# Moving block 0's products with W1 from the preparation into the keys' stage of a graph-attention kernel

## The chip, the cores and the metric

The kernel runs on one core of a Trainium2 chip. The metric is the time of one execution on the device in microseconds (us), the median of three runs. A profiled execution gives the times of single instructions. The engines are named as in the profile: PE (TensorE, matrix products and transposes; PEld is its weight load), DVE (VectorE), ACT (ScalarE), POOL (GpSimd, which issues the gathers) and SP (SyncE, which issues most other transfers). Each engine works through its own list of instructions in order and waits where a semaphore tells it to.

## The reference

Two layers of relational graph attention over a graph of 3125 nodes with 768 features and 53125 edges of three types, then a residual sum and a layer norm. One layer, cut to what matters:

```python
xr = jnp.einsum('nd,rdf->rnf', x, W)          # W: three relations, 768 x 768
oi, oj = xr[etype, dst], xr[etype, src]
alpha = jax.nn.leaky_relu(oi @ q + oj @ k, 0.2)
m = jax.ops.segment_max(alpha, dst, num_segments=n_nodes)
e = jnp.exp(alpha - m[dst])
z = jax.ops.segment_sum(e, dst, num_segments=n_nodes)
a = e / (z[dst] + 1e-16)
msg = (a[:, :, None] * oj.reshape(-1, heads, out_ch)).reshape(-1, heads * out_ch)
out = jax.ops.segment_sum(msg, dst, num_segments=n_nodes) + b
```

Layer 1 has four heads and the weights W1, q1, k1; an ELU follows it. Layer 2 has one head. At the end: `_layernorm(x + out)`. The edges come sorted by their target node.

## The kernel before, in words

The nodes are cut into 25 blocks of 128 (`NB`); the last holds 53 nodes. The edges are cut into slots of 128, at most 14 for block 0 and 17 for every other block, 422 in all (`NK`). A product with float32 accuracy is made of three products of split numbers, so that one "group" (128 nodes by half of one relation's 768 columns) takes 6 x 3 = 18 matmuls. Everything is written under a manual schedule: the order of the program is the order of each engine's list.

The stages:

1. **Preparation** (`prepare`, `weights_kq`, `nodes_kq`). W1 is loaded in 18 pieces of 384 KB, each split into a high and a low part (`wH`, `wL`) and turned on PE (L260) for the product of W1 with q1 and k1, which gives the small matrix `wk` (product L282, placing L320). Then the 25 blocks of x are loaded, turned and multiplied with `wk`, which gives every node's key and query numbers (product L282, placing L372); the keys go to a table in DRAM, `kt1` (L379). Two blocks make one chunk. In before, chunk 0 is block 0 alone, and its turned parts are kept (`t0H`, `t0L`), so that `first` (L396) can make block 0's products with W1 in 18 parts of six matmuls each. `early` and `fills` say how many parts are made at which step. The rows that come of it go from three buffers ("row") to the table `tab1`, by ACT's copies (L403) and ACT's queue (L406). `Buffers` deals six buffers of `share` out to the pieces of W1, the blocks of x and these rows in the order of `waiting`; a load is issued on SP (L173, L178) when a buffer comes free. `prepare` writes the edges' tables in small steps that `more` puts between these.

2. **The keys' stage** (`phase1`). POOL gathers the keys of every slot from `kt1` (L461, 422 gathers of 128 rows). The gathers of one block need its index: a transpose on PE (L540), then DVE (L545 to L570). PE adds the scores' helpers per block (L613, L642, L659), and beside that makes the products of x with W1, group by group (`d_group`, L698), after turning the block (`d_turn`, L675). ACT copies a group's result to a row buffer (L713) and SP stores it to `tab1` (L715). Six groups make one block; the last four blocks go together, relation by relation (the tail), since their turned parts are kept in other buffers. `ev` says at which group number each helper step is done: six groups to a block, with a fixed distance for each step. Every sixth matmul of a group also waits for a certain gather ("an even load"), so that the groups are spread over the gathers. The node blocks come again from DRAM for this, one at a time (`x_load`, one buffer `xr`).

3. **Layer 1's sums** (`phase2`) gather rows from `tab1` and need the whole table. **Layer 2** (`phase3`) follows.

A fallback kernel for other edge lists is in the file, and is not run for these inputs.

Of the kernel before, what the change touches and what calls it, by code (L numbers as in the profile page):

```python
# [8 lines left out]
F32 = mybir.dt.float32  # L9
# [40 lines left out]
def kernel(  # L50
# [95 lines left out]
    class Buffers:  # L146


        def __init__(self):
            w = [("W", i) for i in range(R * DT)]  # L150
            self.waiting = w[:10] + [("x", 0)] + w[10:] + [("x", b) for b in range(1, NB)]
            self.spare = list(range(6))
            self.at = {}

        def __getitem__(self, key):
            t = share[self.at[key]]
            return t if key[0] == "row" else t[:, :D]

        def want(self, *key):
            self.waiting.insert(0, key)  # L160
            self.go()

        def free(self, *key):
            self.spare.append(self.at.pop(key))
            self.go()

        def go(self):
            while self.waiting and self.spare:
                key = self.waiting.pop(0)
                self.at[key] = self.spare.pop(0)  # L170
                kind, i = key
                if kind == "W":
                    nc.sync.dma_start(self[key], l1["W"].rearrange("r (t p) f -> (r t) p f", p=P)[i])  # L173
                elif kind == "x":
                    n = min(P, N - i * P)
                    if n < P:
                        V.memset(self[key], 0.0)
                    nc.sync.dma_start(self[key][:n], x[i * P:i * P + n, :])  # L178
# [162 lines left out]
    def nodes_kq(buf, pre, work, psum, bank, wk, kqs, wH, wL, qq, more, edges_ready):  # L341

        NCH = NB // 2 + 1

        def chunk(m):

            return (2 * m - 1, min(2, NB + 1 - 2 * m)) if m else (0, 1)

        def turn(m):
            b, nb = chunk(m)  # L350
            pts = transposes(psum, [buf["x", b + c] for c in range(nb)])
            for c in range(nb):
                buf.free("x", b + c)
            if m > 1:
                place(m - 2, prod.pop(m - 2))
            return split_parts(work, pts, nb * P, "t" if m else "t0")

# [26 lines left out]

        def first(i):

            g, i = divmod(i, 3)
            r, c = divmod(g, 2)
            if i == 0 and c == 0:
                buf.want("row", r)  # L390
            if i == 0:
                po[g] = psum.tile([P, 512], F32, name="po", bufs=1)
            tH, tL = got[0][i]
            for t in (2 * i, 2 * i + 1):
                for n, (a, w) in enumerate(((tH, wH), (tH, wL), (tL, wH))):
                    T.matmul(po[g][:, :HALF], a[:, t % 2, :], w[:, r * DT + t, c * HALF:(c + 1) * HALF],  # L396
                             start=(t == 0 and n == 0), stop=(t == DT - 1 and n == 2))
            if i < 2:
                return
            o = buf["row", r]  # L400
            if c == 0:
                G.memset(o.rearrange("p (h f) -> p h f", h=H1)[:, :, F1:CW], 1.0)
            S.copy(o.rearrange("p (h f) -> p h f", h=H1)[:, 2 * c:2 * c + 2, :F1],  # L403
                   po.pop(g)[:, :HALF].rearrange("p (h f) -> p h f", h=2))
            if c == 1:
                nc.scalar.dma_start(tab1[:P * R, :].rearrange("(p r) f -> p r f", r=R)[:, r, :], o)  # L406
                buf.free("row", r)

        got = {}
        prod = {}  # L410
        po = {}
        left = iter(range(6 * R))

        def fill(n):
            for _, i in zip(range(n), left):
                first(i)

        def begin(m):

            if m in (-5, 0):  # L420
                got[len(got)] = turn(len(got))
            fill(early.get(m, 0))


        early = {-4: 1, -3: 1, -2: 1, -1: 1, 0: 2, 1: 1}
        yield begin
        fills = [0] + [1] * 12 + [2, 0]
        for m in range(1, NCH + 2):
            if m >= NCH:
                place(m - 2, prod.pop(m - 2))  # L430
            elif m > 1:
                got[m] = turn(m)
            fill(fills[m])
            if 0 <= m - 1 < NCH:
                prod[m - 1] = product(m - 1, got[m - 1])
            more(1)
            if m == NCH - 3:
                edges_ready()
                x_load(pre, 1)
        yield  # L440
# [78 lines left out]
    def phase1(pre, work, psum, wH, wL, qq):  # L519
# [167 lines left out]

        def d_group(n, b, r, c):

            g, k = divmod(n, 6)  # L690
# [1139 lines left out]
```

## Time and profile before

| | us |
|---|---|
| three timed runs | 2191.54, 2200.53, 2206.43 (median 2200.53) |
| the profiled execution: time, span | 2187.15, 2185.4 |
| busy: PE, DVE, ACT, POOL | 1994.7 (91%), 1528.2 (70%), 1358.0 (62%), 1669.4 (76%) |
| preparation, to the first gather of keys | 0 to 126.18 |
| keys' stage, to the first gather of rows | 126.18 to 702.13 |
| layer 1's sums, to the last store to layer 2's table | 702.13 to 1538 |
| layer 2 | 1538 to 2185.4 |

All numbers of stages are from the profiled execution, counted from the start of its span. A line of the order of time gives the start, the duration, the engine, the line of the program, the operation, output<-inputs, the shapes, the count and, in brackets, how long the engine was idle before and what it waited for. A table of windows gives, for each stretch of time, the busy time of each engine with its number of instructions, the clock granted to PE as a share of its full clock, the share of time in which the 16 DMA engines were busy, and what they moved.

### The profile page before, as it was taken

What the parts mean: (1) busy time and instruction counts of PE and PEld (TensorE: products, weight loads), DVE (VectorE), ACT (ScalarE), POOL (GpSimd) and SP (SyncE); (2) the same over time, 40 slices, a digit from 0 to 9 for tenths busy, and PEclk for the clock granted to TensorE, in tenths of its full rate; (3) what the DMA queues carried; (4) which work ended last, traced back from release to release, by engine and by line L of the source; (5) the groups of instructions that cost most, each with busy time, mean ns of one, the idle gap of its engine ahead of it and who ended that gap; (6) DMA issues with size and microseconds to landing.
All of it is one profiled execution on the core that took longest, in us unless ns stands there. A gap on an engine that the chain in (4) does not pass through costs nothing.

```text
span 2185.4 us, 37792 instructions
## 1 busy us (share of the span) xinstructions
PE 1994.7 (91%) x10953; PEld 1736.7 (79%) x10953; DVE 1528.2 (70%) x4159; ACT 1358.0 (62%) x3095; POOL 1669.4 (76%) x1615
## 2 busy tenths in 40 slices
PE   6979999999987799999999999999488989999887
PEld 5979988898887799999999999999255555555555
DVE  6545445455434999999999999996166666766666
ACT  5412112222111788888888888885378879788886
POOL 4257777777777888888888888884677777777774
PEclk8989999999999899999999999999699999999999
DMA  6555545555547987888788888886789899988882
GB/s 176 185 141 173 192 144 156 179 167 167 176 155 223 315 243 239 245 245 248 234 251 247 244 242 244 240 253 201 253 290 303 302 311 308 310 288 297 288 297 91
DMA packets 156844, 506.06 MB, mean 232 GB/s; under 512 B 43875, under 2 KB 57069, under 8 KB 156628
## 3 DMA queue, kind: packets, MB, share of 16 engines
q0 software_dynamic: 81904, 331.52, 50.2%
q1 hardware_dynamic: 64494, 156.04, 20.7%
q10 hardware_dynamic: 10230, 15.98, 2.2%
q8 instruction: 91, 1.49, 0.3%
q14 instruction: 125, 1.02, 0.1%
HBM read 412.55 MB, written 95.69 MB: 233 GB/s over the span
## 4 chain that ended last, share of the span: by engine, by line
PE 52%; DMA 14%; issue 14%; POOL 13%; DVE 4%; ACT 2%; POOLq 0%; DVEq 0%; SPq 0%; ACTq 0%
PE po L949 21%; PE acc L894 13%; POOL kt L461 9%; DMA G<-ftab,ridx 9%; PE acc L1168 8%; PE po L698 4%; DMA kt<-kt,ridx 2%; POOL G L461 2%; PE bank L282 1%; PE pt L260 1%; DVE L L1157 1%; PE po L396 1%; PE pt L924 1%; POOL share L461 1%; ACT H L1146 1%
## 5 line engine op out<-in xcount | busy, mean ns | idle before, releaser
L861 ACT ACTIVATE H<-share,pall 128x193 fp32r<-128x193 f32 x1672 | 616.9, 447 | 91.2 <-PE acc L894 29.6
L875 DVE SCALAR_TENSOR_TENSOR L<-share,pall,H 128x193 fp32r<-128x193 f32 x1672 | 621.0, 437 | 16.5 <-issue 6.6
L949 PE MATMUL po<-wH,hT 128*128 128x386 f32 (+1 forms) x1800 | 529.6, 339 | 0.0
L461 POOL DMA_INDIRECT G<-ftab,ridx x374 | 424.0, 1134 | 114.0 <-issue 57.9
L461 POOL DMA_INDIRECT share<-ftab,ridx x374 | 428.3, 1145 | 80.5 <-DVE L L875 30.9
L461 POOL DMA_INDIRECT kt<-kt,ridx x374 | 396.8, 1061 | 114.2 <-issue 110.1
L698 PE MATMUL po<-wH,xT 128*128 128x384 f32 x1584 | 439.7, 347 | 12.7 <-ACT share L713 4.8
L1168 PE MATMUL acc<-G,selp 128*128 128x386 f32 x868 | 341.5, 519 | 0.0
L949 PEld LDWEIGHTS po<-wH,hT 128*128 128x128 f32 x1800 | 334.4, 189 | 0.6 <-DVE hT L937 0.5
L698 PEld LDWEIGHTS po<-wH,xT 128*128 128x128 f32 x1584 | 292.8, 190 | 19.8 <-ACT share L713 7.0
L949 PE MATMUL po<-wL,hT 128*128 128x386 f32 (+1 forms) x900 | 304.8, 339 | 0.0
L698 PE MATMUL po<-wL,xT 128*128 128x384 f32 x792 | 269.2, 340 | 0.0
L1157 DVE SCALAR_TENSOR_TENSOR L<-G,p,H 128x772 fp32r<-128x772 f32 x205 | 208.2, 1017 | 57.3 <-ACT H L1146 56.9
L713 ACT COPY share<-po 128x384 f32<-128x384 f32 x144 | 67.9, 478 | 278.7 <-PE po L698 275.2
L894 PE MATMUL acc<-H,sel 128*128 128x386 f32 x836 | 224.9, 350 | 12.1 <-POOL sel L863 10.9
L1168 PEld LDWEIGHTS acc<-G,selp 128*128 128x128 f32 x868 | 163.8, 199 | 81.3 <-issue 17.3
L863 POOL TENSOR_SCALAR sel<-frow,fdl 128x128 fp32r<-128x128 f32 x278 | 216.0, 777 | 12.6 <-PE acc L894 1.8
L894 PE MATMUL acc<-L,sel 128*128 128x386 f32 x836 | 217.3, 341 | 0.0
L1146 ACT ACTIVATE H<-G,p 128x772 fp32r<-128x772 f32 x205 | 189.9, 928 | 0.9 <-DVE p L1122 0.8
L949 PEld LDWEIGHTS po<-wL,hT 128*128 128x128 f32 x900 | 169.8, 189 | 0.0
L894 PEld LDWEIGHTS acc<-H,sel 128*128 128x128 f32 x836 | 148.8, 190 | 23.2 <-POOL sel L863 21.1
L894 PEld LDWEIGHTS acc<-L,sel 128*128 128x128 f32 x836 | 154.8, 191 | 0.2 <-DVE L L875 0.2
(246 smaller groups left out, 2810.1 us busy)
## 6 DMA issues: line engine op xcount, KB each, us to landing
ftab<-share SPq DMA_DIRECT2D x75, 386.0 KB
ftab<-r SPq DMA_DIRECT2D x75, 386.0 KB
share<-in_L_gnn_W_dram SPq DMA_DIRECT2D x36, 384.0 KB
w_d<-w2hl SPq DMA_DIRECT2D x18, 768.0 KB
sT<-dr_d SPq DMA_DIRECT2D x25, 544.0 KB
share<-in_x_dram SPq DMA_DIRECT2D x25, 384.0 KB
xb_d<-share SPq DMA_DIRECT2D x25, 384.0 KB
xr<-in_x_dram SPq DMA_DIRECT2D x23, 384.0 KB
```

What stands on the lines that cost most here:

```text
L260: T.transpose(pt[:, f, c * P:(c + 1) * P], a[:, (2 * i + f) * P:(2 * i + f + 1) * P], ident)
L461: return G.indirect_dma_start(out=to, out_offset=None, in_=tab, in_offset=_index(i[:, j:j + 1]), bounds_check=NP * R - 1, oob_is_err=False)
L698: m = T.matmul(po[:, :HALF], xT[:, s, t, :], w[:, i, sl], start=(n == 0), stop=(n == 3 * DT - 1))
L713: S.copy(to, po[:, :HALF].rearrange("p (h f) -> p h f", h=2))
L861: S.activation(H[:, c], g[:, c], AF.Copy, scale=pall[:, b, j, h:h + 1])
L863: (V if k % 3 == 0 else G).tensor_scalar(sel, row, dl[:, b, j:j + 1], None, op0=ALU.is_equal)
L875: V.scalar_tensor_tensor(L[:, c], g[:, c], pall[:, b, j, h:h + 1], H[:, c].bitcast(F32), op0=ALU.mult, op1=ALU.subtract)
L894: T.matmul(acc[:, c, :HW], sel, a[:, c * HW:(c + 1) * HW], start=(j == 0 and i == 0), stop=(k in ends2 and i == 1), skip_group_check=True)
L949: T.matmul(po[:, :wd], hT[:, k, t, :], w[:, r * DT + t, sl], start=(t == 0 and n == 0), stop=(t == DT - 1 and n == 2))
L1146: S.activation(H, g, AF.Copy, scale=p)
L1157: V.scalar_tensor_tensor(L, g, blk[b]["p"][:, j:j + 1], st[k][1].bitcast(F32), op0=ALU.mult, op1=ALU.subtract)
L1168: T.matmul(acc[:, c, :HW], sel, a[:, c * HW:(c + 1) * HW], start=(j == 0 and i == 0), stop=(k in ends and i == len(parts) - 1))
```

## The change

Block 0 is treated like all other blocks. In the preparation `first`, its parts, its kept tiles and its row buffers are gone, the 18 pieces of W1 are loaded first and then the blocks of x, and the chunks are (0, 1), (2, 3), ..., (22, 23), (24), 13 as before. The last node block has a place of its own, `share[7]`, which is cleared at the start; the loads keep their order, so its load is issued after that of block 23, without a buffer to wait for. In the keys' stage there are 150 groups for 144. The helper steps of a block are placed at 37/6 groups per block (`when`) for 6, and the groups are spread over the gathers by one formula, 23/25 of the matmuls' sixths, for a rule by blocks. The special load and sum that made block 0's residual row are gone, since `d_split` now makes it.

```diff
         def __init__(self):
             w = [("W", i) for i in range(R * DT)]
-            self.waiting = w[:10] + [("x", 0)] + w[10:] + [("x", b) for b in range(1, NB)]
+            self.waiting = w + [("x", b) for b in range(NB)]
             self.spare = list(range(6))
-            self.at = {}
+
+            self.at = {("x", NB - 1): 7}
+            V.memset(share[7], 0.0)
...
         def free(self, *key):
-            self.spare.append(self.at.pop(key))
-            self.go()
+            i = self.at.pop(key)
+            if i < 7:
+                self.spare.append(i)
+                self.go()
 
         def go(self):
             while self.waiting and self.spare:
                 key = self.waiting.pop(0)
-                self.at[key] = self.spare.pop(0)
+                if key not in self.at:
+                    self.at[key] = self.spare.pop(0)
...
-        NCH = NB // 2 + 1
+        NCH = (NB + 1) // 2
 
         def chunk(m):
 
-            return (2 * m - 1, min(2, NB + 1 - 2 * m)) if m else (0, 1)
+            return 2 * m, min(2, NB - 2 * m)
...
-        def first(i):
...
         def begin(m):
 
-            if m in (-5, 0):
-                got[len(got)] = turn(len(got))
-            fill(early.get(m, 0))
-
-
-        early = {-4: 1, -3: 1, -2: 1, -1: 1, 0: 2, 1: 1}
+            if m in (0, 1):
+                got[m] = turn(m)
+
         yield begin
-        fills = [0] + [1] * 12 + [2, 0]
         for m in range(1, NCH + 2):
             if m >= NCH:
                 place(m - 2, prod.pop(m - 2))
             elif m > 1:
                 got[m] = turn(m)
-            fill(fills[m])
-            if 0 <= m - 1 < NCH:
-                prod[m - 1] = product(m - 1, got[m - 1])
+            if m - 1 < NCH:
+                prod[m - 1] = product(m - 1, got.pop(m - 1))
             more(1)
             if m == NCH - 3:
                 edges_ready()
-                x_load(pre, 1)
+                x_load(pre, 0)
...
-                        tc.add_manual_dep(m.ins, gathered[g, (3 * k + n // 6) * slots(g) // 18].name, behind,
+                        tc.add_manual_dep(m.ins, gathered[slot((3 * k + n // 6) * 23 // 25)].name, behind,
                                           reason="an even load")
...
-        d_turn(1)
-        d_split(1)
-        x_load(pre, 2)
+        d_turn(0)
+        d_split(0)
+        x_load(pre, 1)
...
-        groups = [(b, r, c) for b in range(1, GB) for r in range(R) for c in range(2)]
+        groups = [(b, r, c) for b in range(GB) for r in range(R) for c in range(2)]
         groups += [(b, r, c) for r in range(R) for b in range(GB, NB) for c in range(2)]
         ev = {}
+
+        def when(b, d):
+
+            return b * 37 // 6 + d
...
-                ev.setdefault(6 * b + d + (b == 1), []).append((f, b))
+                ev.setdefault(when(b, d) + (b == 1), []).append((f, b))
...
-                if 6 * b + d >= 0:
-                    ev.setdefault(6 * b + d, []).append((f, b))
-        ev[6 * NB - 10].append((lambda b: a_last(), 0))
-        for b in range(2, GB + 1):
-            for d, f, o in ((-8, d_turn, 0), (-7, d_split, 0), (-7, x_next, 1)):
+                if when(b, d) >= 0:
+                    ev.setdefault(when(b, d), []).append((f, b))
+        ev[when(NB - 1, -4)].append((lambda b: a_last(), 0))
+        for b in range(1, GB + 1):
+            for d, f, o in ((-2, d_turn, 0), (-1, d_split, 0), (-1, x_next, 1)):
                 ev.setdefault(6 * b + d, []).append((f, b + o))
...
-            if n == 2:
-                nc.sync.dma_start(share[3][:, :D], x[:P, :])
-            if n == 8:
-                V.tensor_add(share[4][:, :D], share[3][:, :D], b2r)
-                nc.sync.dma_start(xb_d[:P, :], share[4][:, :D])
-            m = n - 6 * (GB - 1)
+            m = n - 6 * GB
```

More of the change, by code (lines that the diff above doesn't have):

```diff
@@ L150, in __init__ @@
             w = [("W", i) for i in range(R * DT)]
-            self.waiting = w[:10] + [("x", 0)] + w[10:] + [("x", b) for b in range(1, NB)]
+            self.waiting = w + [("x", b) for b in range(NB)]
             self.spare = list(range(6))
-            self.at = {}
+            self.at = {("x", NB - 1): 7}
+            V.memset(share[7], 0.0)
         def __getitem__(self, key):
[L156 to L160, printed above, removed]
-            self.go()
+            return share[self.at[key]][:, :D]
         def free(self, *key):
-            self.spare.append(self.at.pop(key))
-            self.go()
+            i = self.at.pop(key)
+            if i < 7:
+                self.spare.append(i)
+                self.go()
         def go(self):
@@ L173, in go @@
                     nc.sync.dma_start(self[key], l1["W"].rearrange("r (t p) f -> (r t) p f", p=P)[i])
-                elif kind == "x":
+                else:
                     n = min(P, N - i * P)
-                    if n < P:
-                        V.memset(self[key], 0.0)
                     nc.sync.dma_start(self[key][:n], x[i * P:i * P + n, :])
@@ L355, in turn @@
                 place(m - 2, prod.pop(m - 2))
-            return split_parts(work, pts, nb * P, "t" if m else "t0")
+            return split_parts(work, pts, nb * P)
         def product(m, parts):
@@ L383, in place @@
                                                      g4[:, c, 1, :, 1, :])
-        def first(i):
[L387 to L407, printed above, removed]
         got = {}
         prod = {}
[L411 to L416, printed above, removed]
         def begin(m):
-            if m in (-5, 0):
-                got[len(got)] = turn(len(got))
-            fill(early.get(m, 0))
-        early = {-4: 1, -3: 1, -2: 1, -1: 1, 0: 2, 1: 1}
+            if m in (0, 1):
+                got[m] = turn(m)
         yield begin
-        fills = [0] + [1] * 12 + [2, 0]
         for m in range(1, NCH + 2):
@@ L686, in d_split, with d_group @@
             nc.sync.dma_start(xb_d[b * P:(b + 1) * P, :], xb)
-        def d_group(n, b, r, c):
-            g, k = divmod(n, 6)
+        def d_group(k, b, r, c):
             po = psum.tile([P, 512], F32, name="po", bufs=2)
```

## The prediction

> **What bounds the kernel now.** I read the page first (PE 91% of the span, POOL 76%, the chain half on PE), then the table of engine times by stage, then the order of time of PE and POOL around the two places that the change touches.
>
> The preparation, from PE's order of time (start, duration, engine, line, output<-inputs, count, idle before):
>
> ```profile
> 72.85 1.47 PE L260 MATMUL pt<-fident,share 128*128 128x128 f32 x12
> 74.25 0.32 PE L372 MATMUL bank<-fident,sm 48*128 48x48 f32 x2
> 74.50 0.44 PE L396 MATMUL po<-wH,t0H 128*128 128x384 f32 x1
> ...
> 75.49 0.34 PE L396 MATMUL po<-wH,t0L 128*128 128x384 f32 x1
> 75.66 0.40 PE L282 MATMUL bank<-tH,wk 128*128 128x256 f32 x2
> ...
> 77.05 1.47 PE L260 MATMUL pt<-fident,share 128*128 128x128 f32 x12
> ...
> 114.50 1.42 PE L260 MATMUL pt<-fident,share 128*128 128x128 f32 x11 [2.68 <-DMA share<-in_x_dram]
> 116.54 0.80 PE L282 MATMUL bank<-tH,wk 128*128 128x256 f32 x2 [0.37 <-ACT g L374]
> 117.14 0.63 PE L282 MATMUL bank<-tL,wk 128*128 128x256 f32 x2
> ```
>
> One pair of node blocks takes 4.20 us (72.85 to 77.05) without a gap: turning, placing, one sixth-part of block 0's products (L396, 74.50 to 75.66, 1.16 us), key product. PE is the bound there. At the end PE waits 2.68 us for the last node block's load.
>
> The same stage by windows (us from the start; busy us of PE, PEld, DVE, ACT, POOL; granted clock; DMA share; GB/s):
>
> ```profile
> 40.00:50.00 10.00, 8.84 (x68) 8.37 (x69) 8.23 (x18) 7.24 (x14) 3.92 (x3) 1.00 0.55 169
> 50.00:60.00 10.00, 9.10 (x73) 8.65 (x72) 9.79 (x17) 6.71 (x14) 5.16 (x5) 1.00 0.54 165
> 70.00:80.00 10.00, 10.00 (x75) 9.38 (x74) 5.34 (x13) 5.64 (x15) 2.82 (x8) 1.00 0.48 148
> 90.00:100.00 10.00, 10.00 (x81) 9.56 (x80) 5.07 (x12) 4.90 (x12) 2.32 (x8) 1.00 0.77 235
> 110.00:120.00 10.00, 6.49 (x41) 5.68 (x40) 4.19 (x10) 3.77 (x9) 0.00 (x0) 0.83 0.17 56
> ```
>
> While W1 is split (40 to 60) DVE is 90% busy too; with the node blocks (70 to 110) only PE is full.
>
> The keys' stage, from POOL's order of time, then PE's:
>
> ```profile
> 126.18 1.11 POOL L461 DMA_INDIRECT kt<-kt,rfirst  x1 [19.20 <-DVE own L567]
> ...
> 634.60 1.00 POOL L461 DMA_INDIRECT kt<-kt,ridx  x1 [0.48 <-DVE lim L556]
> ...
> 700.83 1.00 POOL L461 DMA_INDIRECT kt<-kt,ridx  x1 [0.30 <-DMA ftab<-share]
> 702.13 0.99 POOL L461 DMA_INDIRECT share<-ftab,rfirst  x1 [0.30 <-issue]
> ```
>
> ```profile
> 571.62 0.52 PE L642 MATMUL pa<-fident,al 128*68 128x128 f32 x3 [1.07 <-DVE al L636]
> ...
> 627.25 1.51 PE L675 MATMUL px<-fident,xr 128*128 128x128 f32 x6 [8.24 <-DMA xr<-in_x_dram]
> ...
> 706.46 0.83 PE L642 MATMUL pa<-fident,al 128*68 128x128 f32 x3 [7.69 <-DVE al L636]
> ```
>
> POOL issues 422 gathers of keys without a rest, 1.00 us each and 0.30 between, a few longer: 126.18 to 701.83, 1.364 us apiece. That chain is the stage's length; the next stage's first gather follows at once. PE, paced to it, waits now and then for the gathered keys (571.62) and once for a load. So I count in time after the first gather (t0 = 126.18).
>
> **The preparation.** 18 parts leave, 1.16 us each: 20.9 us of PE at most. Term by term:
> - Ten pair periods, turns 2 to 11. Without its part PE needs 3.04 us; DVE 2.14 (0.25 + 1.89), ACT 2.18 (0.24 + 1.57 + 0.37). DMA: shares of 0.57, 0.48, 0.54, 0.77 and 0.49 in the five windows from 60 to 110 make 28.5 us over 12 pairs, 2.4 each. All below PE. But two loads (786 KB) at 235 GB/s, the best of the windows shown, would take 3.35. I take 1.0 us saved per period: **10.0** (0.85 to 1.16: 8.5 to 11.6).
> - Four W1 periods, 4.64 us (45.13 to 49.77). PE would do with 3.48, DVE's 90% are 4.2. Saved 0.45 to 1.16 each; I take 0.6, as DVE is nearer: **2.5** (1.8 to 4.6).
> - From turn 1 to turn 2 (59.05 to 68.69, 9.64 us, four parts). Then this stretch holds the turn of the first pair too (+1.4), and the waits that the parts covered are bare: sums' copies (0.45 each) and wk's four DVE steps (0.8 at 66.34). Say 7.6: **2.0** (1.0 to 2.7).
> - Block 0's six transposes leave the slow spot at 34.48 (18 in 3.90 us there, 12 in 2.6 by 28.54's rate): **1.2**.
> - The end. The last chunk holds one block (0.75 us for 1.47) and its load no longer waits for a buffer: it follows block 23's load instead of the turn of blocks 19 and 20. 111.55 to 115.84 becomes 0.8 to 1.0: **3.3** (0.7 to 3.6). Without the pause the product after it keeps its clock (2.95 us now, 1.40 elsewhere): **1.0** (0 to 1.5).
>
> Sum 20.0 us, t0 at 106; ends 13 and 25. ACT's six copies (0.52 each), three store issues on ACT's queue, POOL's three memsets (0.1) go as well, all beside PE; so do SP's waits for those stores (9.5 us in the queue's waits). New is a 0.70 us memset on DVE, idle until 11 us: nothing.
>
> A rule to weigh: after the pause of 2.68 us a pair of 256-column matmuls took 0.63 us for 0.40, at a granted clock of 0.83 in that window. [...] Were the clock to fall in five W1 chunks (transposes 2.6 for 1.46, product 2.58 for 1.39), the 20.0 would be 8.
>
> **The keys' stage.** PE gets six groups of 18 matmuls, 3.17 us each (668.51 to 671.68), and one turn (0.82): +19.8. ACT gets six copies (0.48) and a cast (0.80), DVE a subtraction (0.94); its addition for xb replaces L802. SP gets three row stores for two transfers of block 0, in a stage where DMA is half idle. On POOL nothing changes: I cost it 0 (-2 to +3 for longer gathers).
>
> Is there room on PE? From 128.75 to 599.02 it did 120 groups, aux work included, in 22.4 us per six without waits (201.70 to 224.09): 448 us, plus 1.5 at a low clock; some 20 us were waits. With 37/6 groups per block a block costs 22.4 + 3.17/6 = 22.9 us against POOL's 17 x 1.364 = 23.2. It fits, barely: PE stays paced. Block 19's last key is gathered at slot 337, t0 + 463, its scores pass PE at group 122; four groups on, the tail (last four blocks) starts at about t0 + 482, where it was t0 + 472.8.
> The tail itself is the same 24 groups with the same 8.24 us stall: its load is issued when block 23's rows are free, in both. It takes 97.6 us (599.02 to 696.6), so PE ends at t0 + 579.5 for t0 + 570.4. Then a copy (0.7), a store's issue (0.35) and its landing (under 3.6 today, as 702.13 didn't wait): the next stage's first gather at t0 + 583.5 for 575.95, 7.5 late. The scores of block 24 hold ACT until 709.73 anyway (first scaling at 710.20, t0 + 584.0), so less of it counts: I take **+6** (0 if the tail's stall shrinks; 18 if the waits stay and all 19.8 come on top).
>
> [...]
>
> **Sum.** -20.0 + 6 = -14 us; the later stages move along. On the profiled execution: 2187.15 - 14 = 2173. That execution lies under all three timed runs (2191.54 to 2206.43); from their median 2200.53 it is **2186.5**.
>
> **Rivals.**
> 1. Forecast, PE freed in front and nearly full behind: -14, 2186.5. Chance 0.50.
> 2. Another engine takes over in front (DVE in the W1 chunks, loads at 3.35 us): -13 + 6 = -7, 2193.5. For it DVE's 9.79 of 10; against it the 5.07 with node blocks. 0.20.
> 3. The tail gives nothing back: PE's waits swallow all: -20 + 0, 2180.5. For it the 20 us of waits; against it that they lie before the tail. 0.13.
> 4. Slower: PE becomes the bound of the keys' stage. Its place is the index transpose (L540) that frees POOL for the next block: it queues behind more groups. It decides once PE's lag exceeds POOL's lead; at 634.60 the lead is used up already (0.48 for 0.30). Then all 19.8 and the store's tail come through POOL, +20 for -13: +7, 2207.5. Against it: block 22's index is now issued ahead of the stalled turn, and 22.9 is under 23.2. 0.11.
> 5. The change doesn't shorten the preparation, because the loads pace it: only the end's 4 us come, +6: +2, 2202.5. Against it: no PE wait for a load from 29 to 111. 0.06.
>
> The bounds run from -25 to +7, with a few us for the runs' own spread: 2172 to 2207. One per cent (22 us) is about what a measurement of this kernel can tell. Faster by more: the low half of case 3 and the edge of 1: 0.15. Slower by more: the far edge of 4: 0.03. Within: 0.82.
>
> **What would show it.** Right: first gather of keys near 106; pair periods near 3.2 us; no wait before the last turn; 422 gathers again in 576 us; an idle stretch of some 6 us on POOL between the last gather of keys and the first of rows. Wrong: pair periods still near 4 with waits for loads; POOL gaps over 0.3 us before a block's first gather, laid to DVE L556; PE waits for keys gone before the tail.

## The result

The changed kernel takes 2203.86 us (median of 20 runs; 2189.62 to 2218.64 but for one slow run of 2770.47, at a granted clock of 0.65), the kernel before 2195.91 us beside it (20 runs, 2184.96 to 2206.43). The ratio is 1.0043, with a 95% interval from 1.0025 to 1.006: **slower by 9 us** (by the ratio; the medians lie 8.0 us apart), where 14 us of gain were forecast. That is under the one per cent that the forecast's chances called no change, but the sign is wrong and the cause can be found. The profiled execution of the changed kernel took 2206.68 us, its span is 2204.9 us, its mean granted clock 0.958 (0.961 before). Before's profiled execution (2187.15 us) lies 8.8 us under its median, so the two profiles lie 19.5 us apart; about 10 us of that are not in the medians, and I compare stages, not whole spans.

POOL's order of time for the changed kernel (start, duration, engine, line, operation, output<-inputs, count, idle before and releaser):

```profile
117.37 1.11 POOL L424 DMA_INDIRECT kt<-kt,rfirst  x1 [13.01 <-DVE own L530]
...
654.01 0.99 POOL L424 DMA_INDIRECT kt<-kt,ridx  x1 [4.57 <-DVE lim L519]
...
678.21 1.44 POOL L424 DMA_INDIRECT kt<-kt,ridx  x1 [2.25 <-DVE lim L519]
...
699.62 0.99 POOL L424 DMA_INDIRECT kt<-kt,ridx  x1 [0.30 <-issue]
...
709.01 1.00 POOL L424 DMA_INDIRECT share<-ftab,rfirst  x1 [8.40 <-DMA ftab<-share]
```

The preparation got shorter by 8.8 us (126.18 to 117.37), not by 20. From the first gather of keys to the first gather of rows it takes 591.6 us, not 575.95: 15.7 us more, where about 7 were forecast. Together the sums of layer 1 start 6.9 us later (702.13 to 709.01). The gathers of keys now wait twice for an index (4.57 and 2.25 us, "DVE lim"), and the first gather of rows waits 8.40 us for the last store of rows, so PE's last group sets the end of the stage.

**The preparation.** PE's order of time, changed kernel:

```profile
55.91 0.80 PE L280 MATMUL bank<-tH,kqs 128*128 128x256 f32 x2 [4.55 <-DVE g L320]
...
99.05 0.50 PE L280 MATMUL bank<-tH,wk 128*128 128x256 f32 x2 [0.46 <-ACT g L372]
...
100.54 1.47 PE L258 MATMUL pt<-fident,share 128*128 128x128 f32 x12
101.94 0.32 PE L370 MATMUL bank<-fident,sm 48*128 48x48 f32 x2
102.72 0.50 PE L280 MATMUL bank<-tH,wk 128*128 128x256 f32 x2 [0.46 <-ACT g L372]
```

A pair of blocks now takes 3.54 to 3.71 us (once 4.45, with a step of the edges' tables in it), not 3.2. After the placing (L370, 101.94) PE has to wait 0.46 us until ACT has copied its result out of the PSUM tile `bank` (L372), since the next product writes other columns of the same tile. In before the part of block 0 stood in just this place (74.50 to 75.66) and covered the copy. The wait at 55.91 is a new one. What DVE and POOL did just before it:

```profile
46.89 0.18 DVE L320 COPY g<-bank 128x32 f32<-128x32 f32 x1
47.10 5.57 DVE L322 TENSOR_TENSOR w<-g 128x16 f32<-128x16 f32 x1
52.71 0.17 DVE L323 CAST wk<-w 128x16 fp32r<-128x16 f32 x1
```

```profile
45.48 0.53 POOL L200 DMA_DIRECT2D dr_d<-share  x1 [4.64 <-DVE share L225]
46.02 6.62 POOL L303 TENSOR_TENSOR wL<-share,wH 128x768 fp32r<-128x768 f32 x4
```

DVE's addition of 128 x 16 numbers lasts 0.18 us elsewhere and 5.57 us here. It ends (52.67) where POOL's run of four subtractions ends (52.64). The copy that PE waited for (L320, at 55.67) stands behind this addition in DVE's list. The run is that long because POOL stood behind a store for 4.64 us and the pieces had piled up. After PE's pause of 4.55 us its granted clock is 0.74 and 0.75 in two windows, and 1.00 in the ones before and after (us from the start; busy us of PE, PEld, DVE, ACT, POOL; granted clock; DMA share; GB/s):

```profile
40.00:50.00 10.00, 8.34 (x68) 7.43 (x68) 9.79 (x17) 8.43 (x17) 5.35 (x5) 1.00 0.52 151
50.00:60.00 10.00, 5.00 (x28) 4.43 (x28) 9.16 (x16) 2.81 (x6) 2.64 (x2) 0.74 0.64 204
60.00:70.00 10.00, 7.90 (x47) 7.31 (x46) 7.13 (x20) 3.68 (x7) 0.00 (x0) 0.75 0.41 141
```

The transposes of one chunk took 2.82 us in that stretch, 1.53 before it.

**The keys' stage.** The longest waits of PE from the first gather of keys to its last group (us in total, times, longest), before:

```profile
PE pa L642 <- DVE al L636: 14.0, 11, 2.1
PE px L675 <- DMA xr<-in_x_dram: 8.9, 2, 8.2
```

and in the changed kernel:

```profile
PE px L638 <- DMA xr<-in_x_dram: 13.0, 2, 7.6
PE po L660 <- ACT share L675: 4.4, 9, 0.8
PE pa L605 <- DVE al L599: 3.9, 5, 1.6
```

The waits for scores ("al") fell from 14.0 to 3.9 us; those for a node block's load rose from 8.9 to 13.0. The turns of the last blocks in PE's order, and the loads on SP's queue, changed kernel:

```profile
595.01 0.82 PE L638 MATMUL px<-fident,xr 128*128 128x128 f32 x6
...
611.36 1.54 PE L638 MATMUL px<-fident,xr 128*128 128x128 f32 x6 [5.42 <-DMA xr<-in_x_dram]
...
620.46 0.87 PE L638 MATMUL px<-fident,xr 128*128 128x128 f32 x6
...
636.56 1.51 PE L638 MATMUL px<-fident,xr 128*128 128x128 f32 x6 [7.59 <-DMA xr<-in_x_dram]
```

```profile
600.30 0.82 SPq L453 DMA_DIRECT2D T<-ed_d  x1
601.33 0.71 SPq L497 DMA_DIRECT2D w<-ed_d  x1
...
602.65 0.37 SPq L468 DMA_DIRECT2D xr<-in_x_dram  x1
...
627.14 0.30 SPq L468 DMA_DIRECT2D xr<-in_x_dram  x1
```

The load for the turn at 611.36 is issued 7.6 us after the turn before it (595.01), the last one 6.7 us after (620.46); before, the last one took 4.5 us (611.49 to 616.03). In the order of the program, index and scan steps stand ahead of that block's split (L646), and only the split frees the buffer. On DVE, where the first of these steps waits for PE:

```profile
599.13 0.22 DVE L541 TENSOR_SCALAR s_all<-pT,s_all 128x1 f32<-128x1 f32 x1 [2.45 <-PE pT L539]
...
600.14 0.94 DVE L646 TENSOR_TENSOR xT<-px,xT 128x768 fp32r<-128x768 f32 x1
```

The late issue is not the whole of the first wait. In before the load for the turn at 603.00 is issued just as late (589.38 to 597.56, 8.2 us), and PE does not wait for it: 13.6 us lie between the two turns there, 2.07 of them a wait for scores, and 10.9 here, without the wait. And here the load itself takes 8.66 us to land, against 4.37 for the next one in before (issued at 606.99). On SP's list it stands right behind two loads of the edges' tables (L453, L497). That these made it slow is not shown.

### The profile page after: what moved, and what is told of

It reads as the page before. It is cut to its first block, busy times and chain, and to the rows that moved or that the text cites. A ratio compares the mean times of both kernels' runs of the same rounds, so it can differ in the third digit from the quotient of the medians.

```text
span 2204.9 us, 37814 instructions
## 1 busy us (share of the span) xinstructions
PE 2003.9 (91%) x10959; PEld 1741.7 (79%) x10959; DVE 1529.6 (69%) x4159; ACT 1358.5 (62%) x3096; POOL 1685.5 (76%) x1613
## 4 chain that ended last, share of the span: by engine, by line
PE 57%; DMA 11%; issue 11%; POOL 10%; DVE 7%; ACT 2%; SPq 0%; POOLq 0%; DVEq 0%; ACTq 0%
PE po L910 19%; PE acc L855 12%; PE acc L1129 10%; PE po L660 9%; DMA G<-ftab,ridx 7%; POOL kt L424 7%; DVE L L836 2%; POOL G L424 2%; PE bank L280 1%; DMA share<-in_L_gnn_W_dram 1%; POOL share L424 1%; PE pt L258 1%; PE pt L885 1%; DMA xr<-in_x_dram 1%; POOL sel L824 1%
## 5 line engine op out<-in xcount | busy, mean ns | idle before, releaser
L836 DVE SCALAR_TENSOR_TENSOR L<-share,pall,H 128x193 fp32r<-128x193 f32 x1672 | 621.8, 436 | 32.8 <-issue 19.3
L660 PE MATMUL po<-wH,xT 128*128 128x384 f32 x1656 | 456.5, 347 | 10.2 <-ACT share L675 4.4
L660 PEld LDWEIGHTS po<-wH,xT 128*128 128x128 f32 x1656 | 306.8, 191 | 16.5 <-ACT share L675 7.9
L660 PE MATMUL po<-wL,xT 128*128 128x384 f32 x828 | 282.2, 341 | 0.0
L660 PEld LDWEIGHTS po<-wL,xT 128*128 128x128 f32 x828 | 158.2, 191 | 0.0
```

The lines of the kernel that those rows point to most:

```text
L836: V.scalar_tensor_tensor(L[:, c], g[:, c], pall[:, b, j, h:h + 1], H[:, c].bitcast(F32), op0=ALU.mult, op1=ALU.subtract)
```

## The experiments

**Theory A:** three waits that the forecast did not charge: the shared PSUM tile; DVE held by POOL's run; in the keys' stage, helper steps that run into the turns of the last blocks and make their loads late. **Theory B:** PE is simply full, the waits only move. The diffs are against the changed kernel unless said.

The first four ran together, on a chip on which every version takes some 12 to 14% longer (before: 2506.95 us there, median of 19 runs). Its windows from 330 to 530 us tell where; first before on the first chip, then e1:

```profile
330.00:530.00 200.00, 186.31 (x1183) 178.18 (x1183) 99.63 (x277) 39.17 (x77) 154.88 (x149) 0.99 0.54 170
```

```profile
330.00:530.00 200.00, 157.34 (x802) 137.69 (x801) 69.50 (x189) 25.84 (x52) 105.96 (x99) 0.82 0.35 111
```

There the keys' stage lasts 833 to 855 us, with PE idle again and again for 1 to 10 us, put down to "issue" or to a row buffer, and POOL waiting, mostly 7 to 14 us, for nearly every block's index. I did not find out why. The kernels with the change (e2, e3) are about 1% faster than before there, which e5 does not bear out on another chip. So from these four I read only the preparation, and single transfers.

**e1, the kernel before without block 0's parts** (against before):

```diff
-            if i == 0:
-                po[g] = psum.tile([P, 512], F32, name="po", bufs=1)
-            tH, tL = got[0][i]
-            for t in (2 * i, 2 * i + 1):
-                for n, (a, w) in enumerate(((tH, wH), (tH, wL), (tL, wH))):
-                    T.matmul(po[g][:, :HALF], a[:, t % 2, :], w[:, r * DT + t, c * HALF:(c + 1) * HALF],
-                             start=(t == 0 and n == 0), stop=(t == DT - 1 and n == 2))
...
-                G.memset(o.rearrange("p (h f) -> p h f", h=H1)[:, :, F1:CW], 1.0)
-            S.copy(o.rearrange("p (h f) -> p h f", h=H1)[:, 2 * c:2 * c + 2, :F1],
-                   po.pop(g)[:, :HALF].rearrange("p (h f) -> p h f", h=2))
+                G.memset(o, 1.0)
```

> Before, with block 0's 18 parts and their six copies left out (block 0's rows of the first table are filled with ones, so its products are missing from the output); nothing of them is added elsewhere. Theory A (the parts covered PE's waits: for ACT's copy out of the shared PSUM bank, 0.46 us a pair, and for DVE held up by POOL's run of subtractions): the first gather of keys comes at about 115 to 118, 8 to 11 us earlier, not 20. Theory B (the parts were PE's own time): it comes at 106 to 108. The keys' stage is unchanged in both, so the whole is 0.4 to 0.5% faster by A, 0.9% by B.

Measured: 2502.37 us (10 runs), ratio 0.9972 (0.9933 to 1.001). The first gather of keys comes at 130.92 us, later than the 126.18 of before, though 20.9 us of PE's work are gone; both theories had it earlier, and both missed. From 84.74 on the pairs take 3.6 to 3.7 us, each with the wait for ACT's copy (0.37 to 0.46). The two pairs ahead of them take 6.06 and 4.76 us, with transposes of 2.78 and 2.68 us for 1.47 in the later pairs. The last block's load, still in its old place, is waited for 5.61 us, and after the wait eleven transposes take 2.61 us, where twelve took 1.47 at 106.72. These last costs theory A had not counted. And the long DVE operations are there too, DVE first, then POOL:

```profile
48.14 3.78 DVE L324 TENSOR_TENSOR w<-g 128x16 f32<-128x16 f32 x1
51.96 2.41 DVE L325 CAST wk<-w 128x16 fp32r<-128x16 f32 x1
```

```profile
47.06 4.83 POOL L305 TENSOR_TENSOR wL<-share,wH 128x768 fp32r<-128x768 f32 x3
51.84 0.73 POOL L395 MEMSET share<- 128x772 f32 x1
52.54 1.79 POOL L305 TENSOR_TENSOR wL<-share,wH 128x768 fp32r<-128x768 f32 x1
```

Both end with POOL's (51.92 and 51.89; 54.37 and 54.33). So taking the parts out is by itself enough to bring the waits of the preparation to light: the parts were cover.

**e2, a PSUM bank of its own for the placing:**

```diff
-            pb = bank[:, 2 * P:]
-            if m >= NCH - 2:
-                pb = psum.tile([P, 2, 2 * P], F32, name="pt0", bufs=2)[:, 0, :]
+            pb = psum.tile([P, 512], F32, name="pb", bufs=1)
```

> After, with the placing of the keys (transposes and ACT's copy) in a PSUM bank of its own, so that the next key product need not wait for that copy. Theory A: the pair period goes from 3.67 to about 3.2 us and the first gather of keys from 117.4 to about 112. Theory B (ACT or the loads set 3.67): the period stays. Later stages unchanged: 5 us or 0.2% faster than after by A.

Measured: 2476.41 us (4 runs), ratio 0.9886 (0.9825 to 0.9948). PE's order of time:

```profile
70.05 0.32 PE L368 MATMUL pb<-fident,sm 48*128 48x48 f32 x2
70.30 0.50 PE L280 MATMUL bank<-tH,wk 128*128 128x256 f32 x2
...
73.22 0.32 PE L368 MATMUL pb<-fident,sm 48*128 48x48 f32 x2
73.47 0.50 PE L280 MATMUL bank<-tH,wk 128*128 128x256 f32 x2
```

The pair period is 3.17 us and the product follows the placing at once. The ten periods take 32.7 us without a wait of 0.88 us for the last load, 10.1 us less than before's 42.9: just the ten that the forecast took. The first gather of keys comes at 110.90 us; in e3, on the same chip without this edit, at 115.50.

**e3 and e4, the last block's loads in two transfers of 48 and 5 rows,** in the changed kernel and in before, wherever the last block of x is loaded:

```diff
-        nc.sync.dma_start(xs[b][:n], x[b * P:b * P + n, :])
+        for a, c in ((0, n // 16 * 16), (n // 16 * 16, n)):
+            if a < c:
+                nc.sync.dma_start(xs[b][a:c], x[b * P + a:b * P + c, :])
```

> After, with each load of the last node block (53 rows) cut into 48 and 5 rows. Theory A (the tail's second stall is this load's 9 us on one DMA engine, and PE's stalls there starve POOL of the index): the load lands in 3 to 5 us, the last turn's wait of 7.6 us falls to 2 to 3, POOL's two index waits (4.6 and 2.3) mostly go, and the first gather of rows comes 5 to 8 us earlier after the first gather of keys. Theory B (PE is simply full): the stall's time comes back as later waits and that distance, 591.6 us, stays within 2.

> Before, with the same cut of the last block's loads. Theory A: the wait before the last turn in the preparation (2.7 us) goes, so the first gather of keys comes 2 to 4 us earlier; in the tail the 8.2 us stall falls to 2 to 3, but POOL's gathers set the stage there, so the first gather of rows stays within 2 us of 576 after the first gather of keys. In all 2 to 4 us faster than before. Theory B (the stall matters to the stage in before too): 5 to 8 us more.

Measured: 2485.64 us (10 runs), ratio 0.9905 (0.9862 to 0.9947), and 2472.71 us (4 runs), ratio 0.9851 (0.9789 to 0.9913). The last load of the keys' stage in e1, whole (SP's queue, then PE), took 8.8 us:

```profile
862.63 0.30 SPq L496 DMA_DIRECT2D xr<-in_x_dram  x1
```

```profile
871.46 1.51 PE L666 MATMUL px<-fident,xr 128*128 128x128 f32 x6 [6.16 <-DMA xr<-in_x_dram]
```

In e3 it is issued at 846.41 and PE turns the block at 849.75: 3.3 us. In e4 the same distance is 3.3 us, and in the preparation before's wait of 2.68 us for the last block is gone. The first gather of keys comes at 119.48 there, 6.7 us earlier than in the first profile of before (2 to 4 were expected); 4.0 us of that lie behind the last turn (108.87 to 119.48, for 111.55 to 126.18). So the load's length goes with how its rows are split. In one transfer its 159 KB took 8.97 us in before's preparation and 11.08 in before's keys' stage, where a whole block of 384 KB took 4.37; from 621.5 to 625.0 us in before, with only this load on its queue (q1), that queue's packets kept 6.3% of the 16 DMA engines busy, about one engine's worth. The split load's share was not taken. What it is worth in time comes with e10. The rest of what e3 and e4 expected, in the keys' stage, cannot be read on this chip.

**The next four** ran together on a chip where the stages run as in the first profiles (before: 2193.9 us there, median of 31 runs).

**e5, the changed kernel again.**

> The changed kernel as it is, beside before and the next three kernels on one chip. Both theories: about 0.4% slower than before (the ratio of the twenty runs was 1.0043), first gather of keys near t0 = 117.4 us, 591 us from there to the first gather of rows, if the chip runs the keys' stage as in the two first profiles (PE busy to 0.97). If it runs it as the chip of the first four experiments did (830 to 855 us for the same stretch), it shows how much of that is the chip, and the ratio to before there should be below 1 as for the other two kernels with this change's preparation.

Measured: 2203.0 us (10 runs), ratio 1.0043 (1.0008 to 1.0078). First gather of keys at 118.52, 589.3 us from there to the first gather of rows; the same long waits (4.57 us for DVE, 5.33 and 7.26 for loads, 4.80 and 2.19 for an index). So two profiles of one kernel differ by 2.4 us in that stretch, and the pattern is no accident of one execution.

**e6, the turns ahead of the helper steps:**

```diff
+        for b in range(1, GB + 1):
+            for d, f, o in ((-2, d_turn, 0), (-1, d_split, 0), (-1, x_next, 1)):
+                ev.setdefault(6 * b + d, []).append((f, b + o))
         chain = ((-6, a_index), (-6, a_index2), (-5, a_gathers), (-5, a_next), (-4, a_next2))
...
-        for b in range(1, GB + 1):
-            for d, f, o in ((-2, d_turn, 0), (-1, d_split, 0), (-1, x_next, 1)):
-                ev.setdefault(6 * b + d, []).append((f, b + o))
         for n in range(max(ev) + 1):
+            m = n - 6 * GB
+            if m in (1, 3, 5):
+                d_turn(GB + 1 + m // 2)
+                d_split(GB + 1 + m // 2)
+                if m < 5:
+                    x_load(pre, GB + 2 + m // 2)
             for f, b in ev.get(n, ()):
                 f(b)
             b, i = divmod(n, 6)
-            m = n - 6 * GB
-            if m in (1, 3, 5):
-                d_turn(GB + 1 + m // 2)
-                d_split(GB + 1 + m // 2)
-                if m < 5:
-                    x_load(pre, GB + 2 + m // 2)
```

> At each step n of the keys' stage the turn, the split and the load of the next block are issued ahead of the index, alpha and scan steps of the same n, instead of behind them; nothing else differs from the changed kernel. Theory A (the helper steps, now 37/6 groups a block against 6 for the turns, run into each other: the split of block 21 and of block 23 stand behind index and scan work, so the last loads are issued 6 to 7 us after their turn instead of 4.5, PE waits 5.42 and 7.59 us for them, the index transposes of the last two blocks come late and POOL waits 4.57 and 2.25 us): the two PE waits fall to 2 to 3 and 5 to 6 us, POOL's waits to under 3 us together, the stretch from the first gather of keys to that of rows from 591 to 585-588 us, the time 3 to 6 us below the changed kernel. Theory B (PE is simply full, the waits only shift the idle time about): the stretch stays at 590-592 us and the time within 2 us.

Measured: 2193.47 us (10 runs), ratio 0.9996 (0.9967 to 1.0024): 9.5 us below e5. The stretch is 581.5 us. PE's turns:

```profile
604.67 0.82 PE L638 MATMUL px<-fident,xr 128*128 128x128 f32 x6
...
613.42 0.85 PE L638 MATMUL px<-fident,xr 128*128 128x128 f32 x6 [1.10 <-DMA xr<-in_x_dram]
...
627.49 0.84 PE L638 MATMUL px<-fident,xr 128*128 128x128 f32 x6 [1.23 <-DMA xr<-in_x_dram]
```

and no gather of keys waits more than 0.4 us after the first. PE's last group ends 576.2 us after the first gather of keys (587.0 in the changed kernel), with PE idle for 23.6 us of it instead of 32.8. Theory A, and more than it asked for. The edit also changes SP's list: the load for the turn at 604.67 now stands ahead of the edges' tables, and PE does not wait for it.

```profile
598.37 0.38 SPq L468 DMA_DIRECT2D xr<-in_x_dram  x1
...
600.04 0.82 SPq L453 DMA_DIRECT2D T<-ed_d  x1
```

What the earlier split and what the new place on SP's list is worth, e6 does not separate. The last load itself still took 9.5 us (617.99 to 627.49). It was issued 4.6 us after the turn before, not 6.7, and PE had 12.8 us to fill between the two turns instead of 8.5, 1.9 of them a wait for gathered keys: the wait partly got shorter and partly got covered.

**e7, the helper steps back at six groups per block:**

```diff
-            return b * 37 // 6 + d
+            return 6 * b + d
```

> The due times of the index, alpha and scan steps of block b go back to 6b + d from 37b/6 + d: one number of the change undone, the rest as changed. The steps then keep one place against the turns for all blocks and are up to four groups earlier at the last blocks; PE's hold on the gathers' count stays as changed. Theory A (drift): POOL's waits of 4.57 and 2.25 us go, PE's waits at the last two turns go back to before's 0.70 and 8.24 us (13.0 to 8.9 us), the stretch falls from 591 to 583-587 us, 4 to 8 us below the changed kernel. Theory B (PE full): POOL ends earlier but PE's last group stays at 587 us after the first gather, the stretch at 590 us or more, the time within 2 us. A third way: the gathers come so early that they wait for the key table's place or for alpha, and POOL's waits get longer than 6.8 us.

Measured: 2205.16 us (10 runs), ratio 1.0065 (1.0037 to 1.0093). The numbers are those of theory B: POOL's waits for an index are gone, its last gather of keys is issued at 689.68, and then

```profile
711.15 1.00 POOL L424 DMA_INDIRECT share<-ftab,rfirst  x1 [20.48 <-DMA ftab<-share]
```

the stretch is 594.3 us, and PE's last group ends 590.1 us after the first gather of keys. PE's waits here:

```profile
PE pa L605 <- DVE al L599: 14.3, 7, 3.4
PE px L638 <- DMA xr<-in_x_dram: 8.4, 1, 8.4
```

So the drift as such was not the fault, and this half of theory A falls. With the old pace PE waits for scores as in before (14.3 us, 14.0 in before), now with six groups more to do; the new pace takes 10 of these 14 us away and gives 4.6 back at the loads. POOL's waits for an index did not set the time: without them it is no shorter, since PE's last group ends the stage. What counts is PE's idle time, and e6 shows that the order of the steps within a group number was the dear part of it.

**e8, two of POOL's subtractions to DVE:**

```diff
-                (V if i % 3 == 2 else G).tensor_sub(wL[:, i, :D], raw[c], wH[:, i, :D].bitcast(F32))
+                (V if i % 3 == 2 or i in (13, 15) else G).tensor_sub(wL[:, i, :D], raw[c], wH[:, i, :D].bitcast(F32))
```

> In front, two of the subtractions that make wL (those of pieces 13 and 15) go from POOL to DVE, nothing else. Theory A (a run of four POOL subtractions, 46.02 to 52.64 us in the changed kernel, holds a DVE addition of 128x16 for 5.57 us since the two engines contend, PE waits 4.55 us for it and then runs at a clock of 0.75 for ten microseconds): the long addition goes, no DVE operation of 128x16 lasts over 2 us there, PE's wait falls from 4.55 to under 1.5 us, the first gather of keys comes at 109 to 113 us instead of 117.4, the time falls by 3 to 8 us. Theory B (the addition is long for its own reason, or DVE with two more subtractions of 1 to 1.7 us becomes the one that PE waits for): the wait stays over 3 us and the first gather of keys within 2 us of 117.4.

Measured: 2197.15 us (10 runs), ratio 1.0016 (0.9985 to 1.0046). That is 5.9 us below e5, but the two intervals overlap; the profile is the surer evidence. The first gather of keys comes at 110.94 us, and the stretch to the first gather of rows takes 592.6 us, as in the changed kernel within 3.3. DVE's longest addition, then what PE waited for it:

```profile
52.81 0.53 DVE L322 TENSOR_TENSOR w<-g 128x16 f32<-128x16 f32 x1
```

```profile
52.83 0.50 PE L280 MATMUL bank<-tH,kqs 128*128 128x256 f32 x2 [0.38 <-DVE g L320]
```

The granted clock is 1.00 in all windows from 40 to 80 us. Theory A: DVE took on 1.9 us of work, and its longest addition went from 5.57 to 0.53 us.

**The last four** ran together again on such a chip (before: 2197.46 us there, median of 35 runs). **e9** is e2, e6 and e8 in one, **e10** e9 with the split loads of e3, **e11** the kernel before with the edits of e6 and e8, **e12** e2 once more.

> Three edits of the changed kernel together: the placing's results get a PSUM bank of their own, the subtractions for pieces 13 and 15 go to DVE, and the turn, split and next load are issued ahead of the helper steps of their n. Theory A (the three waits are separate and add up): first gather of keys at 117.4 - 6.4 (pieces, 110.94 alone) - 4.6 (banks, 110.90 against 115.50 on the other chip) = 105 to 107 us, 580 to 583 us from there to the first gather of rows (581.5 with the order alone), the first gather of rows at 686 to 690 us, the time 10 to 12 us under the 2193.5 of the order alone: 2180 to 2184 us, ratio to before 0.992 to 0.996. Theory B (the front's gain is spent in the keys' stage, which starts earlier but is held by its gathers or by PE at one end): the first gather of keys as in A, the stretch 588 us or more, the time within 4 us of the order alone.

> The kernel of e9 and the load of the last node block in two transfers of 48 and 5 rows. Theory A (with the turns issued first the last turn's wait is 1.2 us though its load takes 9.5 us; what counts is when the load is issued): the load takes 4 to 6 us instead of 9.5, the wait of 1.2 us goes, the stretch shrinks by 0 to 1.5 us, the time within 2 us of e9. Rival (the load over one engine also holds up other transfers of these microseconds, among them the gathers' own): the stretch shrinks by 3 us or more.

> Two of the edits of e9, the two pieces to DVE and the turns ahead of the helper steps, made in the kernel before; the third has no place there, since the products of block 0 lie over the wait for the bank. It tells what the change itself is worth when both versions have the same repairs. Theory A (both faults were brought in or made larger by the change: in the kernel before the POOL run holds a DVE addition for 3.13 us, not 5.57, and the last two turns wait 0.70 and 8.24 us): first gather of keys at 122 to 125 us (126.2), the stretch 573 to 576 us (575.95), the time 1 to 5 us below before, so that e9 is 7 to 13 us faster than this kernel. Rival (the faults are as dear in before, the change is worth nothing by itself): 9 us or more below before, equal to e9 within 3 us.

> The kernel of e2 again, on a chip where the keys' stage runs as in the first profiles, to price the shared bank in time. Theory A: pair period 3.2 us as in e2 (3.55 to 3.7 in the changed kernel), first gather of keys at 112 to 113.5 us (117.4), the stretch 589 to 592 us as in the changed kernel, the time 4 to 6 us below the changed kernel (ratio to before 1.001 to 1.003). Rival (the time goes back into the wait for the last load or into the keys' stage): the first gather of keys earlier but the time within 2 us of the changed kernel.

| | first gather of keys | to the first gather of rows | median us (runs) | ratio to before |
|---|---|---|---|---|
| before, first profile | 126.18 | 575.95 | | |
| e9 | 104.50 | 582.1 | 2184.37 (12) | 0.9943 (0.9921 to 0.9966) |
| e10 | 104.38 | 580.4 | 2182.62 (12) | 0.9932 (0.9907 to 0.9958) |
| e11 | 125.03 | 575.2 | 2195.92 (12) | 0.9993 (0.9974 to 1.0012) |
| e12 | 112.75 | 593.8 | 2201.09 (12) | 1.0019 (0.9993 to 1.0045) |

POOL's two marks in e9:

```profile
104.50 1.11 POOL L422 DMA_INDIRECT kt<-kt,rfirst  x1 [11.35 <-DVE n_all L526]
...
686.61 1.00 POOL L422 DMA_INDIRECT share<-ftab,rfirst  x1 [4.83 <-issue]
```

e9 is nowhere more than 0.5 us outside the ranges of theory A: the three waits add up. It beats both kernels, by 13 us the one before and by 22 us the changed one (ratios 0.9943 and 1.0043). e10 adds nothing that can be told from e9 (the stretch is 1.7 us shorter, 0 to 1.5 by theory A): once the load is issued in time, its length is covered (the last turn comes 9.2 us after the load's issue in e9 and 8.0 in e10, both times without a wait). e11 answers whether the two edits are just good for any version: before gains 1.5 us from them, within its interval; its last turn still waits 7.95 us. So the faults of e6 and e8 became dear by the change, and with them and the shared bank mended the change is worth about 11 us (2195.92 against 2184.37). Part of that another repair of before could have brought: e4 took 4.0 us off the end of its preparation, and e11 does not have that edit; the two together were not run. e12 has the front that theory A gave it, but its stretch of 593.8 us is longer than theory A's 589 to 592; its median is 2 to 3 us under the changed kernel's, 5 us by the ratios, and the intervals overlap, so its worth in time by itself is not shown. Its loads wait 5.40 and 7.79 us like the changed kernel's.

## Why the prediction was wrong

Its own terms (us; minus is gained), with what the changed kernel and e9 showed. The marks are PE's turns of W1 and of the pairs: before at 28.54, 68.69 and 111.55, changed at 29.04, 70.58 and 107.88, e9 at 28.79, 62.74 and 95.86, then the first gather of keys.

| term | forecast | changed | e9 |
|---|---|---|---|
| first W1 turn starts | 0 | +0.5 | +0.25 |
| W1, block 0's transposes, to the second pair's turn | -5.7 (2.5 + 1.2 + 2.0) | +1.4 | -6.2 |
| ten pair periods | -10.0 | -5.6 | -9.7 |
| the end, with its clock | -4.3 | -5.1 | -6.0 |
| preparation | -20.0 | -8.8 | -21.7 |
| keys' stage, to the first gather of rows | +7.5, counted +6 | +15.7 (e5: +13.3) | +6.2 |
| time, by the medians' ratio | -14 | +9 | -12.5 |

**Pair periods, the term "1.0 us saved per period".** PE's need of 3.04 us and the other engines' busy times were right, and e2's 3.17 us shows it. The failed step is that busy times were added up per engine and the chain placing, copy, product was not followed. It could be read in before: placing ends at 74.57, ACT's copy takes 0.24 us, where no part lies over it PE waits 0.37 us for it (the line at 116.54, which the forecast shows), and what stood in between was the very work to be taken away. Price 4.4 us.

**W1 periods and the stretch after them (4.5 us together).** The failed step is "DVE's 90% are 4.2": a share, where a single operation was the limit. The profile of before held its warning, an addition of 3.13 us at 50.17 and a cast of 1.79 us at 41.09, each ending with POOL's subtractions (53.26 and 42.85). POOL stood before the same store in before too (5.05 us, to 47.90), and three subtractions came in one run behind it; with the chunks in closer order there were four, and the hold grew to 5.57 us. With PE's pause came the fall of the clock that the forecast had priced for five W1 chunks, at 12 of its 20.0 us, and not counted: the pause was 4.55 us and the clock 0.74 to 0.75 in two windows, and in e8, where the wait is 0.38 us, it is 1.00 there. e8 takes the run apart and gets 6.4 us back. Two small slips of the working cancel (block 0's transposes 3.90 - 2.6 = 1.3 us, not 1.2; four times 0.6 is 2.4, not 2.5). Rival 2 had this place, DVE in the W1 chunks, but not the reason, and only a small price.

**The end (4.3 forecast, 5.1 measured)** was right: with a buffer of its own the last block's load comes early enough that no wait is left before the last turn. The load itself stays long: in the keys' stage it takes 9.4 us in the changed kernel, and 3.3 us split in two (e3, e4).

**The keys' stage.** The added work was right: PE is busy 554.2 us for 532.0, +22.2 against 19.8. That the new pace would swallow waits for scores was right too, and e7 measures it: 10 us. The failed step is "the tail itself is the same 24 groups with the same 8.24 us stall". The tail had two stalls, 13.0 us. Counted from the first gather of keys, PE's last group ended at 587.0 us, not 579.5. About 4 of these 7.5 us arose in the tail (102 us for 97.6), and about 3 ahead of it: it began at 485 us, not 482, later than the 22.9 us per block had it. The forecast took the distances of the steps for the schedule; which step stands first where two fall on the same group number was not looked at, and with 37/6 against 6 that differs from block to block. e6, which changes only this and with it the place of the loads on SP's list, gives 581.5 us, 2 us less than the 583.5 forecast. Rival 4 named the right sign and the index's lateness on POOL, but e7 shows that POOL's waits were a symptom: without them the stage is as long.

Sum: 4.4 for the bank, 7.1 for DVE's hold, 7.3 to 9.7 in the keys' stage and 0.3 back at the ends make 18.5 to 20.9 of the 23 us between -14 and +9. What the profiles show after the first gather of rows (1483.3 us before, 1495.9 changed, 1498.2 in e5, 1485.7 to 1498.7 in e6 to e12) varies by some ten us between versions with the same code there; that was not looked into, and the rest may lie there.

That the mended kernel e9 comes so near the forecast (-12.5 for -14) is in part luck: in e6 the tail too begins some 2 us late, and then takes 92 us where the forecast had 97.6 with its stall.

## What to carry to other kernels

Work that stands between a producer and a consumer on the bounding engine is cover (here 1.16 us of products over a wait of 0.46 us): before it is taken out, follow the chain under it, the PSUM tile's next writer above all, and price the bare wait. A small operation that lasts many times its usual time (here 5.57 us for 0.18) can be a wait in disguise, so compare its end with the ends on the other engines. And when steps with different periods share one schedule, write out which comes first wherever they meet: here that order was worth 9.5 us, as much as the changed kernel had lost.

## What the runs showed of the hardware

A DVE addition of 128 x 16 numbers lasted 5.57 us, 0.18 us elsewhere, while POOL made four subtractions of 128 x 768 one after the other (46.02 to 52.64). It lasted to the end of the run of four (52.67), not of the one subtraction that was under way at its start (1.66 us each), and 3.13 and 3.78 us with runs of three in before and e1. In e8, with two subtractions moved to DVE, the longest was 0.53 us. What held it is not shown.

On one chip the kernels took 12 to 14% longer, most of it in the keys' stage (833 to 855 us for 575 to 594), at granted clocks of 0.77 to 0.87 over 200 us windows; its cause is open. And from its issue to PE's turn the load of 53 rows took 8.8 to 12.3 us in one transfer, and 3.3 us as 48 and 5 rows (e3, e4, on that chip, where one transfer took 8.8).
